# A Perceiver kernel: the last three running maxima of a half batch ahead of the span attention's minimum on VectorE, and the first block's copy ahead of the deferred steps on ScalarE

## The chip, the cores and the metric

The kernel runs on one core of one Trainium2 chip. The metric is the device time of one execution in microseconds. The time before is the median of three runs. The profile is of one further execution, with a time of its own; every duration below is from that execution.

## The reference, cut to what matters

There are 32 batches of 64 queries with 256 features. Each batch attends to its own 1601 context rows with 16 heads of width 16, then goes through a second, "span" attention over its own 64 positions, then through a hash-routed mixture of small networks:

```python
x = x + xattn(layernorm(x), ctx, ctx, mask)     # softmax over 1601 keys, 16 heads
x = x + span_attn(layernorm(x))                 # below
x = x + ffn(layernorm(x))                       # shared network + 2 of 8 experts per token
# span_attn, per head: mean and soft are made from h @ W_span.T
diff = pos[None, None, :] - mean[..., None]
scores = -soft[..., None] * (diff * diff)       # 64 positions for each of 64 queries
attn = softmax(scores); out = attn @ value
```

Both softmaxes take off a maximum before the exponential. In the span attention the kernel holds soft·diff², so the maximum of the scores is the minimum of that tensor; the kernel calls it `least`.

## The kernel before, in words

A **half** is one batch with 8 of its 16 heads; there are 64 halves, numbered n = 0 to 63, and the loop over them is the main part of the program. The scores of a half lie in SBUF with keys on the partitions, as 13 blocks of 124 keys; for each block there are four pairs of heads, 128 columns each. The 13 blocks are worked in four groups (4, 3, 3 and 3 blocks). The loop is a software pipeline: in turn n the scores of half n+1 are made, the maxima of half n are subtracted, its exponentials are taken, and the products with the values of half n-1 are made. A turn has four **stretches**, one for each group; stretch 4n+g is group g of turn n.

The order of instructions on TensorE, VectorE, ScalarE and GpSimd is the order in which the program issues them (a manual schedule), so moving a call in the source moves its instructions in the queues of exactly those engines that it uses.

In one stretch VectorE adds the mask to four tiles of scores (L504, out of PSUM into `prob`), and between these adds it takes running maxima over blocks that are already there (`maximum`, L525, 124x512, into the PSUM tile `mrun`). The running maximum starts as a copy of block 0, made by ScalarE (`first_maxima`, L517). Blocks 1 to 9 are taken between the adds; blocks 10, 11 and 12 are taken at the end of the turn (`BETWEEN[-1]`, L745), and the last of them writes `mx` instead of `mrun`. At the start of the next turn TensorE turns `mx` (four transposes into `pm`, L532), VectorE reduces that to `mc` (L539), TensorE spreads `mc` over the rows (`pb`, L547), ScalarE copies that to `mb` (L551), and GpSimd subtracts `mb` from each pair of heads (`less_maxima`, L556), 3.7 us each. TensorE's order around this is: scores of group 0 (`psc`, L495), `pm`, one key projection of the next batch (`pk`, L450), `pb`, 104 products with values (`pvs`, L571), scores of group 1.

The span attention of a tile of two batches is a generator, `span_steps`, whose parts are put into an **agenda**: `run(s)` at stretch s runs the next part of every generator due there, and the list `WAITS` says how many stretches later the following part is due. A tile starts every four halves, so each part of it comes at the same place of every fourth turn. In turns 6, 10, 14, ... 62 (15 of them) these parts come up:
- group 0: the small VectorE arithmetic (L279 to L295), which borrows a corner of `mrun` as scratch through `aside`. The first block's copy, L517, overwrites that corner and so must come later.
- group 2: ScalarE's square and GpSimd's product (L304, L305).
- group 3: VectorE's `least` (L308, 128x1024 reduced to 128x16) and GpSimd's subtraction of it (L309).

In the turn after (7, 11, ...) group 0 has ScalarE's exponential of the span scores (L311), and group 1 has VectorE's `total` (L313). In the following turn, group 0 has the transposes and the two copies `aT` (L325); in the one after that, group 0 has the last sum of one tile (`po`, L343 and L346) and the copy `hT` (L228) of the next. ScalarE's `qbd` and the normalisations stand in other groups. The `run` call of group 3 stands before the three last maxima, and the `run` call of group 0 before the first block's copy.

Of the kernel before, what the change touches and what calls it, by code (L numbers as in the profile page):

```python
# [33 lines left out]
BETWEEN = [(), (1, 2, 3), (4, 5, 6), (7, 8, 9), (10, 11, 12)]  # L34
# [40 lines left out]
def perceiver_kernel(ctx: ExitStack, tc: tile.TileContext, a: dict[str, bass.AP], out: bass.AP):  # L75
# [3 lines left out]
    NTILE = NT // P  # L79
# [130 lines left out]
    WAITS = (1, 1, 1, 1, 1, 1, 1, 1, 1, 1, 1, 3, 3, 1, 1, 1)  # L210
    CLOSE = (1, 1, 1, 1, 0, 2, 1, 1, 1, 1, 1, 2, 1, 1, 1, 1)

    def span_steps(t: int, oT):
        waits = iter(CLOSE if t >= NTILE - 2 else WAITS)
        x = xs[t]
        po = mm_bank(f"po_{t}")
        for c in range(2):
# [101 lines left out]
        for q in range(2):  # L319
            ps = mm_bank(f"psa_{t}_{q}")  # L320
            for i in range(4):
                n = 4 * q + i
# [6 lines left out]
        for c in range(2):  # L329
            for b in range(2):  # L330
                for j in range(4):
                    n = 4 * c + j
# [46 lines left out]
    def pair_of(n: int, j: int):  # L379
        return prob[:CHUNK, place(n, j // 2), j % 2]  # L380

    def block_of(n: int, k: int):

        first, last = place(n, 0), place(n, 1)
        return prob[:CHUNK, first : last + 1 : last - first, :, k, :]
# [23 lines left out]
    def query_steps(t: int):  # L409
        spread = spread_of(xs[t], f"q{t}")  # L410
        yield 1
        xn = normalised(xs[t], spread, f"q{t}")
        yield 1
        ps = transposed(xn, f"q{t}")
        xnT = work.tile([P, 2, P], F32, tag="xnT", name=f"xnT_{t}")
        nc.vector.tensor_copy(xnT, ps)
        yield 1
        pq = mm_bank(f"pq_{t}")
        for c in range(2):
            for i in range(2):  # L420
                nc.tensor.matmul(
                    pq[:, c * P : (c + 1) * P], lhsT=wqT[:, i, c * P : (c + 1) * P],
                    rhs=xnT[:, i, :], start=(i == 0), stop=(i == 1),
                )

        q = work.tile([P, 2, 2, 2, S], F32, tag="qbd", name=f"qbd_{t}")
        for c in range(2):
            for e in range(2):
                nc.scalar.activation(
                    q[:, c, :, e, :], pq[:, c * P : (c + 1) * P].rearrange("p (b q) -> p b q", b=2),  # L430
                    AF.Identity, bias=bq4[:, c, e : e + 1], scale=own4[:, e : e + 1],
                )
        qbd[t] = q
        yield 1

        nc.gpsimd.tensor_tensor(xs[t], xs[t], bo_row, ALU.add)

    def load_context(b: int):
        for g in range(len(GROUPS)):
            load_piece(b, g)  # L440
        if b % 2 == 0 and b // 2 + 1 < NTILE:
            t = b // 2 + 1
            load_x(t)
# [72 lines left out]
    def first_maxima(n: int):  # L516
        nc.scalar.copy(mrun[:CHUNK].rearrange("p (r i) q -> p r i q", r=2), block_of(n, 0))  # L517

    def maximum(n: int, k: int):

        dst = mrun
        if k == NKC - 1:
            dst = mxs[n] = work.tile([P, 4, P], F32, tag="mx", bufs=1, name="mx")
        dst, run = (m[:CHUNK].rearrange("p (r i) q -> p r i q", r=2) for m in (dst, mrun))
        nc.vector.tensor_tensor(dst, block_of(n, k), run, ALU.max)  # L525

    def turned_maxima(n: int):

        m = mxs.pop(n)
        ps = mm_bank("pm")  # L530
        for j in range(4):
            nc.tensor.transpose(  # L532
                ps[:, j * CHUNK : (j + 1) * CHUNK], m[:CHUNK, j, :], ident[:CHUNK, :CHUNK]
            )
        return ps, work.tile([P, 4], F32, tag="mc", name="mc")
# [7 lines left out]
    def maxima_along_rows(col):  # L543

        ps = mm_bank("pb")
        for j in range(4):
            nc.tensor.transpose(  # L547
                ps[:CHUNK, j * P : (j + 1) * P], col[:, j : j + 1].to_broadcast([P, CHUNK]), ident
            )
        m = work.tile([P, 4, P], F32, tag="mb", bufs=1, name="mb")  # L550
        nc.scalar.copy(m[:CHUNK].rearrange("p j q -> p (j q)"), ps[:CHUNK])  # L551
        return m

    def less_maxima(n: int, j: int, m, engine):
        sj = pair_of(n, j)
        engine.tensor_tensor(  # L556
            sj, sj, m[:CHUNK, j, None, :].to_broadcast([CHUNK, NKC, P]), ALU.subtract
        )

    def exponentials(n: int, j: int):  # L560
        nc.scalar.activation(pair_of(n, j), pair_of(n, j), AF.Exp)  # L561

    def values(n: int, r: int):

        b, c = halves[n]
        v = vs[b % 2]
        for k in range(NKC):
            kn = min(CHUNK, KEYS - k * CHUNK)
            for j in range(4):
                h = 4 * r + j  # L570
                nc.tensor.matmul(  # L571
                    pvs[32 * j : 32 * j + DK + 1, c, :, r, :],
                    lhsT=v[:kn, k, 8 * c + h, :],
                    rhs=pair_of(n, h // 2)[:kn, k, (h % 2) * S : (h % 2) * S + S],
                    start=(k == 0), stop=(k == NKC - 1), tile_position=(0, 32 * j),
                )
# [51 lines left out]
            nc.vector.scalar_tensor_tensor(at, p3, b3twice[:, hc : hc + 1], act, ALU.add, ALU.mult)  # L628

    agenda: dict[int, list] = defaultdict(list)  # L630

    def run(stretch: int):
        for steps in agenda.pop(stretch, []):
            while (wait := next(steps, None)) == 0:
                pass
            if wait:
                agenda[stretch + wait].append(steps)

    def finish_steps(b: int, stretch: int):

        t = b // 2
        if b % 2 == 0:
            oT[t] = work.tile([P, 2, 2, S], F32, tag="oT", name=f"oT_{t}")
        flat = "p c u r q -> p (c u r q)"
        nc.vector.transpose(turned_pvs.rearrange(flat), pvs.rearrange(flat))
        by_head = turned_pvs.rearrange("p c u r i -> p (c u r) i")
        rec = work.tile([P, 8], F32, tag="rec", name=f"rec_{b}")
        nc.vector.reciprocal(rec, by_head[:, :, DK])
        o = work.tile([P, 8, DK], F32, tag="o", name=f"o_{b}")
        nc.vector.tensor_tensor(  # L650
            o, by_head[:, :, :DK], rec[:, :, None].to_broadcast([P, 8, DK]), ALU.mult
        )
        nc.vector.transpose(oT[t][:, :, b % 2, :], o.rearrange("p (c n) i -> p c (n i)", c=2))
        if b % 2:
            agenda[stretch + 1].append(span_steps(t, oT.pop(t)))
        yield


# [37 lines left out]
    for n, (b, c) in enumerate(halves[:-1]):  # L696
        if c == 0 and b + 1 < B:
            load_context(b + 1)
        if c and b % 2 == 0 and b // 2 + 1 < NTILE:
            agenda[4 * n + 2].append(query_steps(b // 2 + 1))  # L700

        def project(f, *args):
            if b + 1 < B:
                f(b + 1, *args)

        if n:
            values(n - 1, 0)
            exponentials(n - 1, 3)
        for g in range(len(GROUPS)):
            if g == 0:  # L710
                turned = []

                def turn():
                    turned.extend(turned_maxima(n))
                    return turned

                scores(n + 1, g, BETWEEN[g], turn)
                project(project_keys, c, 0)
                m = maxima_along_rows(turned[1])
                less_maxima(n, 0, m, nc.gpsimd)  # L720
                run(4 * n)
                if n:
                    values(n - 1, 1)
                    if c == 0:
                        agenda[4 * n + 1].append(finish_steps(b - 1, 4 * n + 1))
            else:
                scores(n + 1, g, BETWEEN[g])
                project(project_keys, c, g, g == 3)
                if g == 1:
                    project(project_values, 3 * c)  # L730
                elif g == 2:
                    project(project_values, 3 * c + 1)
                else:
                    for u in (5, 6) if c else (2,):
                        project(project_values, u, True)
            if g:
                less_maxima(n, g, m, nc.gpsimd)
                run(4 * n + g)
            for u in extra.get(4 * n + g, ()):
                linear_factor(u)  # L740
            if g == 0:
                first_maxima(n + 1)
            else:
                exponentials(n, g - 1)
        for k in BETWEEN[-1]:  # L745
            maximum(n + 1, k)


    stretch = 4 * last
# [13 lines left out]
    run(stretch + 1)  # L763
    values(last, 1)
    next(finish_steps(B - 1, stretch + 3))
    gate()
    gate()
# [155 lines left out]
```

## Time and profile before

| what | value |
|---|---|
| runs before | median 1583.82 us (1578.76 to 1586.79, three runs) |
| the profiled execution's own time | 1575.67 us |
| its span, first to last instruction | 1573.6 us |
| mean granted TensorE clock | 0.993 |
| TensorE busy, and weight loads | 1499.1 us (95%), 1094.7 us (70%) |
| VectorE busy | 1258.5 us (80%) |
| GpSimd busy | 1121.5 us (71%) |
| ScalarE busy | 895.6 us (57%) |

The first turn begins at about 40 us, and the last maxima of the last half end at 1409.6 us; what follows is the tail with the last tiles and the mixture of networks. A timeline row gives start, duration, engine, line, operation, output<-inputs, shapes and count; in square brackets is the time for which the engine was idle before it, and what ended that. Rows that follow each other on one engine can overlap by about 0.1 us.

### The profile page before, as it was taken

How to read it: one execution, taken by the hardware profiler on the slowest of the kernel's cores; microseconds unless marked ns; L12 is line 12 of the kernel's file. 1: busy time of each engine (PE TensorE's matmuls, PEld its weight loads, DVE VectorE, ACT ScalarE, POOL GpSimd, SP SyncE). 2: the span in 40 equal slices, each digit the busy share in tenths (PEclk: the TensorE clock that was granted, in tenths of full speed). 3: DMA queues.
4: the chain of work that ended last, by engine and by line, in shares of the span. 5: the costliest groups of instructions: out<-in, count | busy, mean ns of one | idle time of the engine just before them, and what ended most of it. 6: DMA issues, size and time to landing. Idle time of an engine off the chain costs nothing.

```text
span 1573.6 us, 61215 instructions
## 1 busy us (share of the span) xinstructions
PE 1499.1 (95%) x27856; PEld 1094.7 (70%) x27856; DVE 1258.5 (80%) x2700; ACT 895.6 (57%) x1229; POOL 1121.5 (71%) x424
## 2 busy tenths in 40 slices
PE   8999999999999999999999999999999999988899
PEld 5677776776767676776767677767767676754587
DVE  4888889888888988898888988898888889884200
ACT  3565656665565656665666656566655656555311
POOL 1777877878687877788786977778786878761710
PEclk9999999999999999999999999999999999999999
DMA  5111111111111111111111111111111111004100
GB/s 167 55 42 43 35 39 38 44 51 44 51 44 51 32 42 35 46 39 44 51 44 52 44 38 35 41 35 44 51 44 52 44 47 33 6 2 155 57 27 27
DMA packets 52066, 73.68 MB, mean 47 GB/s; under 512 B 3812, under 2 KB 51040, under 8 KB 51680
## 3 DMA queue, kind: packets, MB, share of 16 engines
q1 hardware_dynamic: 50992, 69.00, 15.2%
q8 instruction: 218, 3.57, 0.9%
q10 hardware_dynamic: 816, 0.79, 0.1%
q14 instruction: 40, 0.33, 0.1%
HBM read 65.57 MB, written 4.19 MB: 44 GB/s over the span
## 4 chain that ended last, share of the span: by engine, by line
PE 55%; DVE 41%; issue 2%; ACT 1%; POOL 1%; DMA 0%; DVEq 0%; ACTq 0%; POOLq 0%
DVE mrun L525 15%; DVE prob L504 15%; PE pk L450 13%; PE pv L450 11%; PE psc L495 8%; PE pvs L571 8%; PE py L853 4%; PE u L600 3%; PE pm L532 2%; PE ph L835 2%; PE pb L547 1%; DVE mx L525 1%; DVE total L313 1%; DVE least L308 1%; DVE mrun L293 1%
## 5 line engine op out<-in xcount | busy, mean ns | idle before, releaser
L556 POOL TENSOR_TENSOR prob<-prob,mb 124x1664 f32<-124x1664 f32 x252 | 936.5, 3735 | 274.1 <-ACT mb L551 186.2
L504 DVE TENSOR_TENSOR prob<-psc,madd 124x384 f32<-124x384 f32 (+1 forms) x1024 | 568.6, 581 | 146.1 <-PE psc L495 146.1
L525 DVE TENSOR_TENSOR mrun<-prob,mrun 124x512 f32<-124x512 f32 x704 | 483.7, 687 | 3.9
L561 ACT ACTIVATE prob<-prob 124x1664 f32<-124x1664 f32 x256 | 403.3, 1588 | 46.7 <-POOL prob L556 43.7
L450 PE MATMUL pk<-ct,wkT_sb 128*32 128x361 f32 (+2 forms) x1768 | 406.0, 499 | 8.0 <-DMA wkT_sb<-in_wkT 5.4
L450 PE MATMUL pv<-wvT_sb,ct 128*124 128x256 f32 x3524 | 390.9, 379 | 0.0
L450 PEld LDWEIGHTS pv<-wvT_sb,ct 128*124 128x124 f32 x3524 | 273.5, 132 | 119.8 <-issue 16.8
L465 ACT ACTIVATE kT<-pk,cols 128x372 f32<-128x372 f32 (+2 forms) x256 | 151.9, 593 | 224.8 <-PE pk L450 224.6
L495 PE MATMUL psc<-qbd,kT 32*124 32x128 f32 x6656 | 267.9, 284 | 12.1 <-DVE prob L504 8.5
L495 PEld LDWEIGHTS psc<-qbd,kT 32*124 32x124 f32 x6656 | 214.3, 181 | 65.6 <-DVE prob L504 26.4
L450 PEld LDWEIGHTS pk<-ct,wkT_sb 128*32 128x32 f32 (+1 forms) x1768 | 159.0, 145 | 117.8 <-issue 53.1
L482 ACT COPY v<-pv 124x512 f32<-124x512 f32 (+1 forms) x224 | 124.8, 557 | 202.6 <-PE pv L450 202.4
L571 PE MATMUL pvs<-prob,v 124*17 124x64 f32 x13312 | 212.5, 220 | 1.1 <-issue 0.9
L571 PEld LDWEIGHTS pvs<-prob,v 124*17 124x17 f32 x13312 | 195.7, 98 | 21.1 <-issue 10.8
L532 PE MATMUL pm<-cst,mx 124*128 124x124 f32 x256 | 41.1, 284 | 38.5 <-DVE mx L525 38.0
L517 ACT COPY mrun<-prob 124x512 f32<-124x512 f32 x64 | 38.5, 602 | 59.5 <-DVE soft L295 56.4
L855 DVE SCALAR_TENSOR_TENSOR ot<-py,prob 128x256 f32<-128x256 f32 x16 | 6.8, 425 | 75.7 <-PE py L853 75.7
L600 PE MATMUL u<-xfT,sw_sb 128*128 128x512 f32 x128 | 61.4, 630 | 1.3 <-ACT vbd L262 0.9
L532 PEld LDWEIGHTS pm<-cst,mx 124*128 124x128 f32 x256 | 26.8, 142 | 48.4 <-DVE mx L525 29.6
L547 PEld LDWEIGHTS pb<-cst,mc 128*124 128x124 f32 x256 | 30.0, 136 | 36.1 <-DVE mc L539 25.5
L600 PEld LDWEIGHTS u<-xfT,sw_sb 128*128 128x128 f32 x128 | 25.0, 203 | 30.6 <-issue 26.2
L525 DVE TENSOR_TENSOR mx<-prob,mrun 124x512 f32<-124x512 f32 x64 | 43.9, 686 | 2.2
(126 smaller groups left out, 1128.9 us busy)
## 6 DMA issues: line engine op xcount, KB each, us to landing
ct<-in_ctxT SPq DMA_DIRECT2D x64, 372.0 KB, 3.2
ct<-in_ctxT SPq DMA_DIRECT2D x32, 496.0 KB, 3.6
ct<-in_ctxT SPq DMA_DIRECT2D x32, 361.0 KB, 3.2
w<-in_w SPq DMA_DIRECT2D x16, 256.0 KB, 5.9
x<-in_x SPq DMA_DIRECT2D x16, 128.0 KB, 2.6
x_kept<-x SPq DMA_DIRECT2D x16, 128.0 KB, 2.4
prob<-x_kept SPq DMA_DIRECT2D x8, 256.0 KB, 6.1
out<-ot SPq DMA_DIRECT2D x16, 128.0 KB, 1.9
```

Of the source, the lines that this page charges most:

```text
L450: nc.tensor.matmul(out[at:end], lhsT=lhsT[:, at:end], rhs=rhs, start=start, stop=stop, **(dict(tile_position=(0, at)) if tiled else {}),)
L465: nc.scalar.activation(kTs[c][:, k0 : k0 + kn], ps[:, :kn], AF.Identity, bias=cols[:, B_K + c : B_K + c + 1])
L482: nc.scalar.copy(vs[b % 2][:kn, 2 * u : 2 * u + n, :, :DK], ps[:kn, : n * D].rearrange("p (n h d) -> p n h d", n=n, d=DK),)
L495: nc.tensor.matmul(ps[:CHUNK, k * P : (k + 1) * P], lhsT=kTs[c][32 * j : 32 * j + 32, at : at + CHUNK], rhs=qbd[b // 2][32 * j : 32 * j + ...
L504: nc.vector.tensor_tensor(pair_of(n, j)[:, c0 : c0 + nb, :].rearrange("p k (e q) -> p k e q", e=2), ps[:CHUNK, : nb * P].rearrange("p (k e ...
L525: nc.vector.tensor_tensor(dst, block_of(n, k), run, ALU.max)
L532: nc.tensor.transpose(ps[:, j * CHUNK : (j + 1) * CHUNK], m[:CHUNK, j, :], ident[:CHUNK, :CHUNK])
L556: engine.tensor_tensor(sj, sj, m[:CHUNK, j, None, :].to_broadcast([CHUNK, NKC, P]), ALU.subtract)
L561: nc.scalar.activation(pair_of(n, j), pair_of(n, j), AF.Exp)
L571: nc.tensor.matmul(pvs[32 * j : 32 * j + DK + 1, c, :, r, :], lhsT=v[:kn, k, 8 * c + h, :], rhs=pair_of(n, h // 2)[:kn, k, (h % 2) * S : ( ...
L600: nc.tensor.matmul(ps, lhsT=w[:, c, hc * P : (hc + 1) * P], rhs=xfT[:, c, :, slot], start=(c == 0), stop=(c == 1),)
L853: nc.tensor.matmul(py, lhsT=x, rhs=w, start=(n == 0), stop=(n == len(terms) - 1))
```

## The change

Two calls move. The three last maxima (`BETWEEN[-1]`) now come inside group 3, ahead of `less_maxima` and `run(4 * n + 3)`, instead of after the exponentials. The first block's copy (`first_maxima`) now comes ahead of `run(4 * n)` and of the second half of the value products, except in those turns whose group 0 uses the scratch corner of `mrun`; a set `held_at` remembers them. `finish_steps` fills that set when it puts a tile's generator into the agenda, by summing the tile's first six waits.

```diff
+    SMALL = 6
+
+    def waits_of(t: int):
+        return CLOSE if t >= NTILE - 2 else WAITS
...
-        waits = iter(CLOSE if t >= NTILE - 2 else WAITS)
+        waits = iter(waits_of(t))
...
+    held_at: set = set()
...
             agenda[stretch + 1].append(span_steps(t, oT.pop(t)))
+            held_at.add(stretch + 1 + sum(waits_of(t)[:SMALL]))
...
                 less_maxima(n, 0, m, nc.gpsimd)
+                if 4 * n not in held_at:
+                    first_maxima(n + 1)
                 run(4 * n)
...
+            if g == 3:
+                for k in BETWEEN[-1]:
+                    maximum(n + 1, k)
             if g:
                 less_maxima(n, g, m, nc.gpsimd)
                 run(4 * n + g)
...
             if g == 0:
-                first_maxima(n + 1)
+                if 4 * n in held_at:
+                    first_maxima(n + 1)
             else:
                 exponentials(n, g - 1)
-        for k in BETWEEN[-1]:
-            maximum(n + 1, k)
```

In the built program this changes the following, and nothing else in any queue. On VectorE, in 15 places, the sequence "maximum of block 9, `least`, maxima of blocks 10, 11, 12" becomes "maxima of blocks 9, 10, 11, 12, `least`". On ScalarE, in 43 places, the copy L517 passes ahead of its neighbours: 15 times ahead of `hT` (L228), 14 times ahead of the span exponential (L311), and 14 times ahead of the two copies `aT` (L325). The orders on TensorE, GpSimd and the DMA queue stay as they are.

## The prediction

> **What bounds the kernel now.** I read the page's chain of waits first, then the timeline around one place where an order changes, then the granted clock around several of them. The chain:
>
> ```profile
> PE 55%; DVE 41%; issue 2%; ACT 1%; POOL 1%; DMA 0%; DVEq 0%; ACTq 0%; POOLq 0%
> ```
>
> TensorE and VectorE take turns; ScalarE and GpSimd are almost never what the end waits for. So a moved ScalarE instruction is free unless it is made late by more than its slack, and a moved VectorE instruction counts where VectorE hands over to TensorE. One of the 15 places (the maxima of half 39, timeline of all engines):
>
> ```profile
> 879.44 1.21 DVE L308 TENSOR_REDUCE least<-sc 128x16 f32<-128x1024 f32 x1
> ...
> 880.56 1.42 DVE L525 TENSOR_TENSOR mrun<-prob,mrun 124x512 f32<-124x512 f32 x2
> 882.01 0.69 DVE L525 TENSOR_TENSOR mx<-prob,mrun 124x512 f32<-124x512 f32 x1
> 882.51 1.90 POOL L309 TENSOR_TENSOR sc<-sc,least 128x1024 f32<-128x1024 f32 x1
> ...
> 882.61 1.28 DVE L504 TENSOR_TENSOR prob<-psc,madd 124x512 f32<-124x512 f32 x2
> ...
> 882.75 0.64 PE L532 MATMUL pm<-cst,mx 124*128 124x124 f32 x4 [1.74 <-DVE mx L525]
> ...
> 883.23 1.83 PE L450 MATMUL pk<-ct,wkT_sb 128*128 128x496 f32 x4
> ...
> 883.81 0.67 DVE L539 TENSOR_REDUCE mc<-pm 128x4 f32<-128x496 f32 x1
> ...
> 884.90 0.60 PE L547 MATMUL pb<-cst,mc 128*124 128x128 f32 x4
> ...
> 886.14 1.07 ACT L311 ACTIVATE sc<-sc 128x1024 f32<-128x1024 f32 x1
> 886.33 7.41 POOL L556 TENSOR_TENSOR prob<-prob,mb 124x1664 f32<-124x1664 f32 x2 [1.92 <-ACT mb L551]
> ...
> 887.10 0.60 ACT L517 COPY mrun<-prob 124x512 f32<-124x512 f32 x1
> ...
> 887.96 1.02 DVE L504 TENSOR_TENSOR prob<-psc,madd 124x384 f32<-124x384 f32 x2 [2.29 <-PE psc L495]
> ```
>
> TensorE stands idle for 1.74 us because `mx` is behind `least`. The wait is the same to 0.01 us in all 14 places inside the loop (maxima of halves 7, 11, ... 59). But look at what follows: `mc` has its own condition on VectorE (two adds before it), and `pb` needs it.
>
> **The maxima ahead of the minimum.** Without `least` in between, the same four maxima look like this (half 37):
>
> ```profile
> 834.59 2.14 DVE L525 TENSOR_TENSOR mrun<-prob,mrun 124x512 f32<-124x512 f32 x3
> 836.77 0.69 DVE L525 TENSOR_TENSOR mx<-prob,mrun 124x512 f32<-124x512 f32 x1
> 837.37 1.28 DVE L504 TENSOR_TENSOR prob<-psc,madd 124x512 f32<-124x512 f32 x2
> ```
>
> From the first maximum's start to the end of `mx` it is 836.77 + 0.69 - 834.59 = 2.87 us; with `least` it is 882.70 - 878.84 = 3.86 us. So `mx` comes 0.99 us earlier and `pm` starts at about 881.76. `pk` then ends at 884.07 instead of 885.06. That is not the gain. The next thing late is `mc`: VectorE still does the four maxima, `least`, two adds and then `mc`, in whatever order. Its sum even grows. A maximum that depends on the one before starts 0.72 us after it (three in 2.14 us and the next at 2.18); `least` depends on none of them and starts 0.60 us after one. With `least` in the middle, the step to the first add is 882.61 - 878.84 = 3.77 us; after the change it is the 2.78 us of half 37 (837.37 - 834.59) plus the step of `least`, 880.56 - 879.44 = 1.12, together 3.90. So `mc` ends 0.13 us later, at 884.61. Where `pb` really waits for `mc`, at half 62, it ends 0.77 us after it:
>
> ```profile
> 1387.88 0.67 DVE L539 TENSOR_REDUCE mc<-pm 128x4 f32<-128x496 f32 x1
> ...
> 1388.69 0.62 PE L547 MATMUL pb<-cst,mc 128*124 128x128 f32 x4 [1.53 <-DVE mc L539]
> ```
>
> (1389.31 against 1388.54 within rounding.) So `pb` ends at 884.61 + 0.77 = 885.38 instead of 885.50: 0.12 us gained, and the value products, the scores of group 1 and VectorE's add at 887.96 move by as much. In 14 places: **1.7 us**. The idle time of TensorE is not gone: 0.75 us of it stays before `pm` (881.76 against the 881.01 at which the scores ended) and 0.7 us comes to stand before `pb` (884.76 against 884.07).
>
> [...]
>
> What else hangs on `least`: GpSimd's L309 behind it starts at 882.9 (`least` then ends at about 882.8) instead of 882.51 and ends 0.4 us later; the subtraction queued behind it waits for `mb` anyway, with 1.92 us of idle time, so this is covered down to 1.5 us. The span exponential L311 on ScalarE, now at 886.7, comes 1.9 us after that. `least` itself waits for L305, which ended at 878.86. Cost nothing.
>
> The fifteenth place is the end of the loop (half 63): TensorE idles 3.59 us before `pm` at 1409.74, no `pk` is there, and `mc` waits for `pm`. There the 0.99 us of `mx` passes through to `mb` and the chain behind: **1.0 us**, between 0 and 1.1 (the clock there is at half, and which rows fall under it may shift).
>
> **The copy ahead of the steps.** The copy takes 0.60 us, needs the four adds of group 0 (done at 885.67 here) and follows `mb`, which ends at 886.25. Its reader is VectorE's first maximum at 888.90, which did not wait. So nothing is gained by having it earlier. What it delays: L311 by 0.6 us, to 887.8, read by `total` at 891.62 (3.8 us of slack); `hT`, which waits for TensorE 0.37 us in half 37 while the copy now fills that gap, by about 0.1; the two `aT` copies by 0.6, whose reader on TensorE comes three stretches later. If a bank of PSUM that `hT` or `aT` free were wanted at once, the cost would be up to 0.6 us in 29 places, 17 us; but at half 40 the late `aT` would end at 907.75 (now 907.15) and the next scores start at 907.87, and `hT` has over 1 us. I take 0 for the 43 places.
>
> **The clock.** The last view is the granted clock in windows:
>
> ```profile
> core 0: us, PE busy (x) PEld busy (x) DVE busy (x) ACT busy (x) POOL busy (x), PEclk, DMA share, GB/s
> ...
> 1054.40:1057.80 3.40, 1.66 (x65) 1.36 (x53) 3.33 (x6) 1.43 (x2) 3.40 (x2) 1.00 0.02 5
> 1057.80:1061.20 3.40, 3.40 (x8) 1.84 (x8) 2.76 (x5) 1.26 (x1) 1.50 (x1) 0.50 0.00 0
> ...
> 1231.90:1235.30 3.40, 1.66 (x37) 1.33 (x30) 3.33 (x6) 1.42 (x2) 3.40 (x2) 1.00 0.02 5
> ```
>
> After one of the 14 waits (half 47) TensorE ran at half clock for 3.4 us; `pk` took 3.25 us instead of 1.83, and `pb` came 3.84 us after `pm` instead of 2.15: **1.69 us** lost. The same wait at 1231.9, lying elsewhere in its window, cost nothing. [...] The half-clock stretches of this trace (1057.8, 1409.4, 1436.7 and 1464.0 us) do lie whole multiples of 3.41 us apart; but the gap that preceded the first was 1.74 us. [...] With the change the longest idle time there is 0.75 us, less than the 0.81 us before `pm` in half 37 and its like, after none of which the clock fell; a window that catches both new gaps has about 1.3 us of idle time in its 3.41 and so 2.1 us busy, against 1.66 now. So the falls inside the loop should go.
>
> How many there are in another run depends on where its windows lie. Places follow each other by 87.06 us (882.70 - 795.64), 25.5 windows. A fall adds 1.69 us, which makes 88.75 us, 26.0 windows: the next place then meets the same part of a window, and can fall again. So one run may have one fall and another a row of them. The median run is 1583.82 - 1575.67 = 8.15 us above the profiled one, which is 4.8 such falls, and the three runs differ by 8.0 us among themselves. I can't see these runs, so this is an inference.
>
> **The sum.** Against the profiled execution: 1.7 + 1.0 + 1.7 = 4.4 us, so a span of 1569.2 and, with the 2.07 us around it, 1571.3 us. Against the median: 1583.82 - 2.7 = 1581.1 without falls, less 1.69 for each fall in the median run. With four falls, between the one seen and the six that would explain all of the 8 us, it is 1574.4. I forecast **1574 us**.
>
> **The rivals.**
> - Falls are rare in every run, and the 8 us between profile and runs are something else that stays. For it: 13 of 14 waits passed at full clock. Against it: the spread of the runs. Gain 2.7 to 4.4 us: 1579.4 to 1581.1 us, say 1580.
> - The change does nothing at all: `pb` waits for `mc` as long as it did for `pk`, and falls come elsewhere. This needs 0.12 us more on `mc`. 1583.8 us.
> - Slower: the gap before `pm` of 0.8 us in the halves 9, 13, ... 61 starts to let the clock fall, because removing the larger falls leaves the windows lying badly for all of them. Price 1.69 us each; it decides once it happens more than about six times a run beyond today's falls (2.7 + 7.9 us = 6.3 x 1.69). With all 14: 1583.8 - 2.7 + 23.7 = 1604.8; with eight, 1594.6. Against it: none fell in the profile.
>
> **How the numbers follow.** I give the forecast 0.50, the first rival 0.36, no effect 0.07, slower 0.07. About 0.5% (7.9 us) is what a measurement of this kernel can tell from no change. The forecast needs a median of 1575.9 or less for that; with three falls it is just missed (2.7 + 5.1 = 7.8), so I count 0.45 of it as faster and 0.05 within; with the rivals, within 0.5% is 0.48 and slower 0.07. The forecast's own range is 1571 to 1577; with the first rival and no effect it reaches from 1570 to 1584.
>
> **What would show it.** Right: TensorE's wait for `mx` drops from 1.74 to about 0.75 us in the 14 places, a wait of about 0.7 us for `mc` appears before `pb`, VectorE's idle time before the group 1 add goes from 2.29 to about 2.2, no half-clock window lies between 100 and 1400 us, and the runs after differ by less than 8 us. Wrong: half-clock windows still in the loop, `mc` ending earlier than reckoned, a wait for L517's neighbours on TensorE, or `total` waiting for L311.

## The result, and the profile after

The changed kernel takes 1568.69 us (median of six runs, 1565.35 to 1572.28). The kernel before, run beside it and together with the runs shown above, takes 1582.78 us (1578.76 to 1587.61). The ratio is 0.9908, with a 95% interval of 0.9884 to 0.9932. In a second comparison, described below, it is 0.9951 (0.9932 to 0.9969). The direction was forecast; the time lies 1.3 us below the forecast range of 1570 to 1584 us. The later comparisons have more runs and give smaller differences, 7.5 us for the changed kernel and 9.2 us for the moved maxima alone: a good part of the first one's 14.1 us comes from its runs of the kernel before, which lie high.

The profiled execution after takes 1565.35 us, its span is 1563.2 us: 10.4 us less than before. The page's chain of waits and two of its groups after, and behind them the first of the groups before:

```profile
PE 53%; DVE 43%; issue 2%; ACT 1%; POOL 1%; DMA 0%; DVEq 0%; POOLq 0%; ACTq 0%
...
L537 PE MATMUL pm<-cst,mx 124*128 124x124 f32 x256 | 40.3, 280 | 23.6 <-DVE mx L530 23.5
...
L552 PE MATMUL pb<-cst,mc 128*124 128x128 f32 x256 | 39.4, 277 | 10.9 <-DVE mc L544 10.9
```

```profile
L532 PE MATMUL pm<-cst,mx 124*128 124x124 f32 x256 | 41.1, 284 | 38.5 <-DVE mx L525 38.0
```

(Lines of the code are 5 to 11 further down: `maximum` is L530, `least` L313, `mc` L544, `pb` L552, the first block's copy L522.) TensorE's idle time before `pm` fell from 38.5 to 23.6 us in total, and the wait for `mc` before `pb` grew from 2.3 to 10.9 us. The same place as before, half 39, in the timeline (first the row of before that the distances below start from, then the changed kernel):

```profile
878.84 0.69 DVE L525 TENSOR_TENSOR mrun<-prob,mrun 124x512 f32<-124x512 f32 x1
```

```profile
876.94 2.14 DVE L530 TENSOR_TENSOR mrun<-prob,mrun 124x512 f32<-124x512 f32 x3
...
879.12 0.69 DVE L530 TENSOR_TENSOR mx<-prob,mrun 124x512 f32<-124x512 f32 x1
879.72 1.21 DVE L313 TENSOR_REDUCE least<-sc 128x16 f32<-128x1024 f32 x1
879.86 0.64 PE L537 MATMUL pm<-cst,mx 124*128 124x124 f32 x4 [0.76 <-DVE mx L530]
...
881.01 1.90 POOL L314 TENSOR_TENSOR sc<-sc,least 128x1024 f32<-128x1024 f32 x1 [0.37 <-DVE least L313]
882.05 0.66 DVE L544 TENSOR_REDUCE mc<-pm 128x4 f32<-128x496 f32 x1
...
882.76 0.65 PE L552 MATMUL pb<-cst,mc 128*124 128x128 f32 x4 [0.59 <-DVE mc L544]
...
884.17 3.73 POOL L561 TENSOR_TENSOR prob<-prob,mb 124x1664 f32<-124x1664 f32 x1 [1.25 <-ACT mb L556]
...
885.87 1.02 DVE L509 TENSOR_TENSOR prob<-psc,madd 124x384 f32<-124x384 f32 x2 [1.97 <-PE psc L500]
```

The wait before `pm` is 0.76 us, and 0.59 us of wait stands before `pb`. From the start of the first maximum to the end of `mc` it is 5.77 us (882.71 - 876.94) against 5.64 before (884.48 - 878.84), 0.13 us more; to the end of `pb` it is 6.47 against 6.66, 0.19 less. From the maxima of half 35 to those of half 39 it is 86.85 us (879.80 - 792.95) against 87.06 (882.70 - 795.64): a place is worth 0.21 us (0.20 by the unrounded times).

The granted clock in two long windows, first of the kernel before, then of the changed one (columns: stretch, its length, busy time of the five engines with their instructions, clock, DMA share, GB/s):

```profile
100.00:1400.00 1300.00, 1250.34 (x25432) 917.83 (x25431) 1139.12 (x2460) 791.75 (x1077) 1020.82 (x353) 1.00 0.15 42
1400.00:1562.00 162.00, 148.75 (x1042) 104.83 (x1041) 47.48 (x100) 55.25 (x85) 50.28 (x45) 0.95 0.19 62
```

```profile
100.00:1400.00 1300.00, 1256.20 (x25486) 917.94 (x25488) 1144.62 (x2469) 794.88 (x1080) 1025.92 (x355) 1.00 0.15 42
1400.00:1562.00 162.00, 146.79 (x1038) 106.75 (x1026) 44.22 (x94) 51.69 (x81) 45.45 (x43) 0.99 0.20 65
```

In the tail the clock is 0.95 before and 0.99 after. A **fall** is a stretch in which the clock is at half; the trace's clock records show it in windows of 3.41 us. Before, one such window lies in the loop and five in the tail; after, none in the loop and one in the tail.

So the 10.4 us of the two profiles divide as follows. The last `mx` ends at 1403.78 instead of 1409.59 us, 5.8 us earlier: 14 x 0.21 = 2.9, one fall in the loop 1.7, and 1.0 from the wait at the end of the loop (2.60 us instead of 3.59), which makes 5.6. That the sum fits so well is in part luck: from `mx` of half 7 to that of half 59, what the 13 periods of four halves take above the shortest of them, apart from the fall, comes to 3.9 us before and 4.0 after, but to 6.9 in a second profile of the changed kernel, which has no fall in the loop either. The tail after it takes 159.4 instead of 164.0 us, 4.6 less. The runs below say which of this belongs to the change.

### The profile page after: what moved, and what is told of

Its sections match the earlier page's. It is cut to its first block, busy times and chain, and to the rows that moved or that the text cites. A ratio compares the mean times of both kernels' runs of the same rounds, so it can differ in the third digit from the quotient of the medians.

```text
span 1563.2 us, 61201 instructions
## 1 busy us (share of the span) xinstructions
PE 1494.7 (96%) x27856; PEld 1089.8 (70%) x27856; DVE 1259.5 (81%) x2700; ACT 895.3 (57%) x1229; POOL 1121.7 (72%) x424
## 4 chain that ended last, share of the span: by engine, by line
PE 53%; DVE 43%; issue 2%; ACT 1%; POOL 1%; DMA 0%; DVEq 0%; POOLq 0%; ACTq 0%
DVE prob L509 16%; DVE mrun L530 15%; PE pk L455 11%; PE pv L455 11%; PE pvs L576 8%; PE psc L500 8%; PE py L864 4%; PE u L605 2%; PE ph L846 2%; PE pb L552 2%; PE pm L537 1%; DVE least L313 1%; DVE total L318 1%; DVE mc L544 1%; DVE mrun L298 1%
## 5 line engine op out<-in xcount | busy, mean ns | idle before, releaser
L530 DVE TENSOR_TENSOR mrun<-prob,mrun 124x512 f32<-124x512 f32 x704 | 483.6, 687 | 4.4
L522 ACT COPY mrun<-prob 124x512 f32<-124x512 f32 x64 | 38.2, 598 | 59.3 <-DVE soft L300 56.2
L537 PE MATMUL pm<-cst,mx 124*128 124x124 f32 x256 | 40.3, 280 | 23.6 <-DVE mx L530 23.5
L552 PEld LDWEIGHTS pb<-cst,mc 128*124 128x124 f32 x256 | 28.7, 135 | 48.1 <-DVE mc L544 41.2
L605 PE MATMUL u<-xfT,sw_sb 128*128 128x512 f32 x128 | 57.9, 600 | 1.3 <-ACT vbd L267 0.9
L552 PE MATMUL pb<-cst,mc 128*124 128x128 f32 x256 | 39.4, 277 | 10.9 <-DVE mc L544 10.9
L530 DVE TENSOR_TENSOR mx<-prob,mrun 124x512 f32<-124x512 f32 x64 | 44.0, 687 | 2.2
```

What stands on the lines that cost most here:

```text
L537: nc.tensor.transpose(ps[:, j * CHUNK : (j + 1) * CHUNK], m[:CHUNK, j, :], ident[:CHUNK, :CHUNK])
L552: nc.tensor.transpose(ps[:CHUNK, j * P : (j + 1) * P], col[:, j : j + 1].to_broadcast([P, CHUNK]), ident)
L605: nc.tensor.matmul(ps, lhsT=w[:, c, hc * P : (hc + 1) * P], rhs=xfT[:, c, :, slot], start=(c == 0), stop=(c == 1),)
```

## Experiments

Two theories stood against each other. By the theory of the clock, most of the gain in the median comes from falls of TensorE to half clock that follow the 1.74 us wait for `mx`, and the order itself gives 4 us. By the rival, the order on VectorE, or the copy, gives the gain and the clock is incidental. Kernels that were measured together share the runs of the kernel before.

### The three maxima alone

```diff
+            if g == 3:
+                for k in BETWEEN[-1]:
+                    maximum(n + 1, k)
             if g:
                 less_maxima(n, g, m, nc.gpsimd)
...
-        for k in BETWEEN[-1]:
-            maximum(n + 1, k)
```

> The three last maxima move ahead of the minimum; the copy on ScalarE stays where it was. If the copy is worth nothing, as the prediction says: the whole gain of the change, a ratio to the kernel before of 0.991 (0.988 to 0.993). If the copy carries a part of the gain: between 0.993 and 1.000. In the profile the wait before pm in the 14 places is 0.76 us and the idle time before the group 1 add 1.97 us, as in the changed kernel.

Measured: 1569.40 us (11 runs) against 1578.61 (31 runs), ratio 0.9941 (0.9922 to 0.9961). The wait before `pm` is 0.76 us (once 0.75) in the 14 places, and no window of the loop was at half clock. The ratio forecast for it was too far down, because the kernel before is faster in these runs than in the six above; the median is within 0.7 us of the changed kernel's.

### The copy alone

The edit is the change without the two hunks on `BETWEEN[-1]`:

```diff
                 less_maxima(n, 0, m, nc.gpsimd)
+                if 4 * n not in held_at:
+                    first_maxima(n + 1)
                 run(4 * n)
...
             if g == 0:
-                first_maxima(n + 1)
+                if 4 * n in held_at:
+                    first_maxima(n + 1)
```

> The copy on ScalarE moves; the maxima stay behind the minimum. If the copy is worth nothing: 0.999 to 1.001, the wait before pm stays at 1.74 us in all 14 places, and half-clock windows in the loop stay possible. If the copy carries a part of the gain: 0.993 to 0.998.

Measured: 1579.37 us (14 runs) against 1578.61, ratio 1.0003 (0.9983 to 1.0023). The copy is worth nothing. The waits stayed at 1.74 to 1.75 us, and this profile caught three falls in the loop, each directly after such a wait:

```profile
184.60:188.00 3.40, 3.40 (x8) 1.93 (x9) 2.81 (x5) 1.29 (x1) 1.52 (x1) 0.50 0.04 10
273.30:276.70 3.40, 3.40 (x8) 1.93 (x9) 2.82 (x5) 1.42 (x1) 1.66 (x1) 0.51 0.00 0
1235.90:1239.30 3.40, 3.40 (x8) 1.89 (x8) 2.77 (x5) 1.36 (x1) 1.60 (x1) 0.50 0.00 0
```

Eight matmuls fill each of these windows, most of them the last transposes and the key projection, at a clock of 0.50 to 0.51.

### The order of before, with the wait filled

```diff
         ps = mm_bank("pm")
+        for _ in range(3 if n % 4 == 3 and 7 <= n < 60 else 0):
+            nc.tensor.matmul(ps[:, :D], lhsT=ident, rhs=wvT[:, 0, :], start=True, stop=True)
```

> The kernel before, with three more matmuls of 128x256 on constants put on TensorE ahead of the four transposes into pm in the 14 places (about 1.3 us of its 1.74 us wait); they write what the transposes overwrite. The order on VectorE stays. Theory of the clock (falls to half clock after these waits make most of the gain in the median): mx, pm and the group 1 add stay at the same distance from each other as before, no half-clock window lies between 100 and 1400 us, and the time falls by 4 to 7 us, a ratio of 0.996 to 0.9975. Rival (the order on VectorE makes the gain, the clock little): 0.9995 to 1.001, or slower by the matmuls if they delay pm.

Measured: 1571.63 us (13 runs) against 1578.61, ratio 0.9957 (0.9936 to 0.9978), just past the far end of what was expected (0.996). TensorE in its timeline, at half 39:

```profile
881.34 1.56 PE L532 MATMUL pm<-wvT_sb,cst 128*128 128x256 f32 x6
883.15 0.64 PE L534 MATMUL pm<-cst,mx 124*128 124x124 f32 x4 [0.25 <-DVE mx L525]
883.63 1.83 PE L450 MATMUL pk<-ct,wkT_sb 128*128 128x496 f32 x4
885.30 0.60 PE L549 MATMUL pb<-cst,mc 128*124 128x128 f32 x4
```

Useless matmuls stand in the wait, and `pb` still comes 2.15 us after `pm`, as before; VectorE's wait in group 1 is still 2.29 us. No step of the work is earlier at such a place, yet the kernel is 7.0 us faster, and its profile has no half-clock window in the loop. That is the theory of the clock.

### One matmul in place of three

```diff
-        for _ in range(3 if n % 4 == 3 and 7 <= n < 60 else 0):
+        for _ in range(1 if n % 4 == 3 and 7 <= n < 60 else 0):
```

> The kernel before with one constant matmul in place of three in the 14 waits, which leaves about 1.3 us of the 1.74 us idle. Half 5 of the loop waits 1.16 us and never fell in a profile. If a wait of 1.3 us is also too short to fall after: the same as with three matmuls, a ratio of 0.996, and a granted clock of 0.995 to 0.999. If it still falls at some positions: between 0.997 and 1.000 and a clock between.

Measured: 1570.95 us (21 runs) against 1577.56 (25 runs), ratio 0.9954 (0.9936 to 0.9971), the granted clock 0.994 to 0.999 (mean 0.996). The lower end is 0.001 outside what was expected. What is left of the wait:

```profile
881.24 0.70 PE L532 MATMUL pm<-wvT_sb,cst 128*128 128x256 f32 x2
883.06 0.64 PE L534 MATMUL pm<-cst,mx 124*128 124x124 f32 x4 [1.12 <-DVE mx L525]
```

So a wait of 1.12 us does no harm here and one of 1.74 us can.

Which of the 1.74 us waits are followed by a fall can be read from the traces. Within one trace the falls begin whole multiples of 3.413 us apart, so they give a grid of windows. The profiles of the kernel before and of the copy alone hold 28 such waits: the four that ended 3.23 to 3.30 us into a window were followed by a fall, and the 24 that ended anywhere from 0.08 to 2.77 us into one were not. Here are two waits of the kernel before, one of each kind (the falls of that profile begin at 1057.82 and 1409.40 us; the waits end 3.23 and 2.59 us into their windows):

```profile
1057.64 0.95 PE L532 MATMUL pm<-cst,mx 124*128 124x124 f32 x4 [1.74 <-DVE mx L525]
...
1234.49 0.64 PE L532 MATMUL pm<-cst,mx 124*128 124x124 f32 x4 [1.74 <-DVE mx L525]
```

TensorE is busy for 1.66 us in both windows (the rows in the prediction), so it is not the busy time alone that decides; why the place in the window does is open. With one matmul in the wait, three waits of 1.12 us ended 3.16, 3.18 and 3.32 us into a window, and no fall followed: these passed by their shorter wait, not by a luckier place.

### The minimum taken twice

```diff
+        if t < NTILE - 2:
+            nc.vector.tensor_reduce(small("again"), sc, AX.X, ALU.min)
         nc.vector.tensor_reduce(least, sc, AX.X, ALU.min)
```

> The kernel before with the span minimum taken twice in the 14 places (the first result is not used), so that mx is 1.12 us later and TensorE waits about 2.86 us. The order alone costs 14 x 1.12 = 15.7 us, since pm, pk and pb follow mx. Theory of the clock: a longer wait falls at more positions of the window, so 8 to 14 places of a run fall instead of about 4, at 1.4 to 1.7 us each: 1599 to 1611 us, and a granted clock of 0.980 to 0.987 instead of 0.992. Rival (the falls do not depend on this wait): 1592 us at the clock of the kernel before.

Measured: 1608.97 us (5 runs) against 1577.56, ratio 1.0178 (1.0129 to 1.0226), 31.4 us more, of which the order explains 15.7. The clock of its runs is 0.977 to 0.985. In the profile 10 of the 14 waits, now 2.86 us each, were followed by a fall, three of them by two windows. The first of these:

```profile
core 0: us, PE busy (x) PEld busy (x) DVE busy (x) ACT busy (x) POOL busy (x), PEclk, DMA share, GB/s
269.30:272.70 3.40, 1.29 (x48) 1.00 (x36) 3.34 (x4) 1.34 (x2) 3.40 (x2) 1.00 0.02 5
272.70:276.10 3.40, 2.64 (x7) 1.67 (x8) 3.39 (x6) 1.15 (x1) 1.39 (x1) 0.50 0.00 0
276.10:279.50 3.40, 3.40 (x43) 1.98 (x45) 0.35 (x1) 1.37 (x3) 0.04 (x1) 0.50 0.16 20
```

With 1.12, 1.74 and 2.86 us of wait the profiles of the order of before had 0, then 1 and 3, then 10 places with a fall, of 14. The rival's 1592 us is 10 us below the fastest run.

### The changed kernel again, and the wait at the end of the loop

Four kernels ran together: the changed kernel; the kernel before with its 14 waits filled and seven matmuls in the 3.6 us wait at the end of the loop; the changed kernel with five matmuls in its 2.6 us wait there; and one more, told last. The edit of the second; the third has `5 if n == last else 0` as its count:

```diff
+        for _ in range(7 if n == last else 3 if n % 4 == 3 and n >= 7 else 0):
+            nc.tensor.matmul(ps[:, :D], lhsT=ident, rhs=wvT[:, 0, :], start=True, stop=True)
```

> The changed kernel itself, beside the following ones. If a whole number of half-clock windows at about 1.7 us each makes the difference from run to run: its slowest and fastest runs lie under 8 us apart, at granted clocks of 0.994 to 0.999, and no half-clock window of its profile lies between 100 and 1400 us. Ratio 0.991 to 0.995. Rival (a gain that has nothing to do with the clock): the ratio does not depend on the clocks of the runs of the kernel before.

Measured: 1568.71 us (15 runs, 1563.94 to 1572.97) against 1576.17 (48 runs, 1568.70 to 1586.81), ratio 0.9951 (0.9932 to 0.9969). The range of 9.0 us is wider than the 8 expected; the clocks are 0.994 to 0.999, as expected, and the loop has no half-clock window.

> The kernel before with constant matmuls in the 14 waits of the loop (three each) and in the 3.6 us wait at the end of the loop (seven). It keeps the order on VectorE and takes away both kinds of long idle time on TensorE. Theory of the clock: the half-clock windows that follow 1409 us go or become fewer too; the time is 1 to 4 us below the filled loop alone, about 1567 to 1570 us. Rival: the same as with the filled loop alone, 1571.6 us.

Measured: 1571.25 us (22 runs), ratio 0.9958 (0.9943 to 0.9973). That is the rival's answer: filling the end of the loop adds nothing to the filled loop (1571.63). The fall at 1409 us is gone from its profile, but four half-clock windows begin at 1427, 1437 and 1465 us all the same.

> The changed kernel with five constant matmuls in its 2.6 us wait at the end of the loop. Its loop has no falls, so what it is below the kernel before with both waits filled is the order alone: 14 x 0.21 + 1.0 = 3.9 us by the profile. Against the changed kernel: 1 to 3 us faster if the tail's half-clock windows begin at that wait, nothing if they begin later.

Measured: 1568.24 us (17 runs), ratio 0.9951 (0.9933 to 0.9969). It is 3.0 us below the kernel before with both waits filled, against 3.9 reckoned. Two kernels without falls in the loop and with the end filled differ by the order alone; so the order is worth about 3 us (the spread of these runs leaves about 1 to 5). TensorE at the end of the loop, first with the order of before, then with the changed one:

```profile
1409.51 0.64 PE L534 MATMUL pm<-cst,mx 124*128 124x124 f32 x4 [0.29 <-DVE mx L525]
1410.92 0.65 PE L549 MATMUL pb<-cst,mc 128*124 128x128 f32 x4 [0.77 <-DVE mc L541]
```

```profile
1402.19 0.64 PE L539 MATMUL pm<-cst,mx 124*128 124x124 f32 x4 [0.15 <-DVE mx L530]
1403.91 0.65 PE L554 MATMUL pb<-cst,mc 128*124 128x128 f32 x4 [1.07 <-DVE mc L546]
```

In the changed order `least` stands between `mx` and `mc` here too: `pb` starts 1.72 us after `pm` instead of 1.41. So 0.3 of the 1.0 us gained at `mx` is given back, 0.7 is left at the end of the loop, and the order comes to 14 x 0.21 + 0.7 = 3.6 us by the profiles. In this comparison, then, the medians go from 1576.17 to 1571.25 us by filling the waits and to 1568.24 by the order: 4.9 us for the falls and 3.0 for the order.

The filling of the end itself, 0.5 us, is less than was expected and less than these runs can tell. It does act on the clock: in all nine profiles that leave the wait there as it is, 2.60 or 3.59 us, a fall began in it or behind it (before at 1409.40 us, 0.34 us ahead of its end; after at 1405.82 us, 1.90 us behind its end), and in none of the three that fill it. But those three have other falls later in the tail.

The granted clock was taken with every run. Over the 104 runs of the kernel before that were made beside these kernels, time and clock have a correlation of -0.94; the fitted line is 1.40 us for each 0.001 of clock. One window of 3.41 us at half clock is 0.0011 of the mean over 1575 us, so a fall costs about 1.5 us by the line; 1.69 us was read at half 47. The means by clock, with the changed kernel's 21 runs beside:

| granted clock of the run | before: runs, mean time | changed: runs, mean time |
|---|---|---|
| 0.997 and up | 12, 1571.9 us | 10, 1567.1 us |
| 0.994 to 0.996 | 24, 1574.2 us | 11, 1570.5 us |
| 0.991 to 0.993 | 32, 1577.8 us | none |
| 0.985 to 0.990 | 36, 1583.1 us | none |

At equal clock the changed kernel is 3.7 to 4.8 us faster; the rest of the gain is that runs at low clock no longer occur. The mean clock is 0.9922 over the 104 runs and 0.9964 over the 21: about four half-clock windows fewer.

### The minimum behind `mc`

The waits within the changed kernel, so that `least` comes in group 0 of the next turn, after the four adds (the span exponential and `total` come one stretch later with it):

```diff
-    WAITS = (1, 1, 1, 1, 1, 1, 1, 1, 1, 1, 1, 3, 3, 1, 1, 1)
+    WAITS = (1, 1, 1, 1, 1, 1, 1, 1, 2, 1, 1, 2, 3, 1, 1, 1)
```

> The changed kernel, with the span minimum put one stretch later, into group 0 of the next turn, behind the four adds and mc (waits of 2, 1, 1, 2 in place of 1, 1, 1, 3 around it), for the tiles 0 to 13. If mc behind the minimum is what keeps the gain of a place at 0.2 us, then here mx and mc are both about 1 us earlier than before: the add of group 1 comes 0.99 us earlier than in the kernel before, 0.78 us earlier than in the changed one, 10.9 us in 14 places: a ratio of 0.984 to 0.985 to the kernel before. If something else (GpSimd, whose subtraction of the minimum now stands between two of its subtractions of mb, or the products' order) sets the place, the ratio stays at 0.990 or worse.

Measured: 1563.92 us (6 runs, 1558.50 to 1566.85) against 1578.61, ratio 0.9908 (0.9878 to 0.9938). It beats both kernels, but the ratio is the one expected if something else sets the place. Against the maxima alone, measured beside it, it is 5.5 us less, half of the 10.9 expected. VectorE at the same place:

```profile
877.42 0.69 DVE L530 TENSOR_TENSOR mx<-prob,mrun 124x512 f32<-124x512 f32 x1
...
881.00 1.21 DVE L313 TENSOR_REDUCE least<-sc 128x16 f32<-128x1024 f32 x1
...
883.37 1.02 DVE L509 TENSOR_TENSOR prob<-psc,madd 124x384 f32<-124x384 f32 x2 [1.16 <-PE psc L500]
...
887.41 1.02 DVE L509 TENSOR_TENSOR prob<-psc,madd 124x384 f32<-124x384 f32 x2 [0.29 <-PE psc L500]
```

From the end of `mx` (878.11) to the group 1 add it is 5.26 us, as in the kernel before (887.96 - 882.70), with `mx` 0.99 us earlier: so the full 0.99 us is there, and `least` lies in VectorE's idle time. In the next group VectorE meets TensorE, which has the scores only 0.29 us later. From that add to the next half's `mx` it takes 14.97 us (898.34 - 883.37) instead of 14.59 (902.55 - 887.96), so 0.38 us are given back, 0.29 of them in this wait. Since `total` has left this stretch of VectorE for the next, where it still takes its 1.2 us, the wait may belong to the moved `total` as much as to the moved minimum; no run parts the two. A period is 86.43 us: 0.62 below before, 0.42 below the changed kernel, about 5.8 us in 14 places.

The same, with five constant matmuls at the end of the loop as above:

```diff
+        for _ in range(5 if n == last else 0):
+            nc.tensor.matmul(ps[:, :D], lhsT=ident, rhs=wvT[:, 0, :], start=True, stop=True)
```

> The minimum behind mc, and five constant matmuls in the wait at the end of the loop. By the profiles 14 x 0.43 = 6.0 us below the changed kernel with the same filling; about 1558 to 1561 us, a ratio of 0.986 to 0.989 to the kernel before.

Measured: 1563.39 us (5 runs), ratio 0.9906 (0.9871 to 0.9940), 2.4 us above what was expected and the same as without the filling within what these runs can tell. Against the changed kernel with the same filling (1568.24) it is 4.9 us less, of the 6.0 expected.

## Why the prediction was right or wrong

**The maxima ahead of the minimum: right, and slightly too small.** That the gain would stop at `mc`, that `mc` would end 0.13 us later, and that the wait before `pm` would be 0.75 us, all came out to 0.01 us. The term that was mis-sized is "ends 0.77 us after it", taken from half 62: from the end of `mc` to the end of `pb` it is 0.70 us in these places. Of the 0.09 us by which the place is better than forecast (0.21 instead of 0.12), that explains 0.07; the rest is within rounding. Over 14 places it is 2.9 instead of 1.7 us. The 0.13 us comes from the two steps in the rows, 0.72 us behind a maximum that the next one needs and 0.60 us behind one that `least` does not need; had they been equal, `mc` would not have moved.

**The end of the loop: right for `mx`, wrong behind it.** The wait for `mx` shrank by 0.99 us, as forecast. That all of it "passes through to `mb`" failed: `mc` waits for `least` there as in the other places, and 0.7 us is left.

**The copy: right.** No gain, no loss: 1.0003.

**The clock: right in its cause, wrong in its size.** The falls in the loop went, as forecast. That the busy time of a window decides, as the comparison of 2.1 with 1.66 us has it, was an estimate and was not shown; what the runs show is the length of the wait and its place in the window. The step that failed is "With four falls, between the one seen and the six that would explain all of the 8 us, it is 1574.4". The base of that sum, 1583.82 us, and the number of falls were not free of each other. The 104 later runs of the kernel before have a median of 1577.4 us, and only 22% of them are as slow as 1582.78; so the three runs lay at the slow end. That they held more falls than usual is inferred from this, since their clocks are not on record. With the 5.8 falls that their distance from the profile implied, the same sum gives 1583.82 - 2.7 - 9.8 = 1571.3; with the 3.6 us of order it is 1570.4, inside the changed kernel's runs and 1.7 us above their median. For the usual run, four falls were right: the clocks of the later runs say about four. Against those runs, 8.7 us (1577.4 - 1568.7) were gained, and the forecast 9.4 (four falls at 1.69 and 2.7 of order) is close to that, in part by luck: the order was taken too small and the fall, at 1.5 us by the fitted line, too dear. I lowered an inference by a third and kept the base that it came from.

**The tail: not forecast.** Of the two profiles' difference, 4.6 us lie in the tail, with five half-clock windows before and one after. The profiles do not give this to the change: that of the maxima alone, with the same order in the tail, has four such windows, the changed kernel's second profile one, and the kernel before with a filled loop one. How the windows fall in the tail differs from run to run.

**The rivals.** That falls are rare is refuted by the clocks of the runs; that nothing happens, by both ratios. The slower case did not come: in no profile of the changed order did the clock fall after a wait of 0.8 us.

**The windows' regularity** (a fall at one place makes the next place meet the same part of a window) was argued from the distances 25.5 and 26.0. It came out once in four. Of the four falls in the loops of the two profiles with 1.74 us waits, one was followed by a fall at the next place, 26.0 windows later (184.59 and 273.34 us with the copy alone). After the other three the next wait came 89.1 instead of 88.75 us later, ended about 0.2 us into a window, and no fall followed. That the falls come at one place of the window is seen in these traces; that they come in long rows is not.

## What to carry to other kernels

- Before a median is taken as the base of a sum, ask what differs from run to run, and put the base and the assumed cause at the same point: here the granted clock of a run told its time with a correlation of -0.94.
- A wait of TensorE had a second price here beside its length: at half 47, where the clock fell after 1.74 us of wait, `pb` came 1.69 us later. Filling the waits with useless matmuls took 4.9 us off the median, the reordering of the work on the path 3.0, so look at the clock behind a wait too.
- When an instruction is moved off a hand-over, look for the next hand-over on the same engine. Behind `mx` stood `mc`, and 0.8 of the 1.0 us was lost there; with `least` out of its way, 0.4 was lost in the next group.

## What the runs showed of the hardware

- A wait of TensorE of 1.74 us was followed by 3.41 us at half clock in 4 of 28 places, with the same instructions around it: in those where it ended 3.23 to 3.30 us into a 3.41 us window, and in none where it ended up to 2.77 us into one. Of 14 waits of 1.12 us none was followed by a fall, of 14 waits of 2.86 us ten were.
- Filling the 14 waits of 1.74 us with matmuls on constants, down to 0.25 us each, made the kernel 7.0 us faster; at a place without a fall no step of its work was earlier.
- On VectorE a 124x512 maximum of 0.69 us that reads the result of the one before started 0.72 us after it (kernel before, half 37: three in 2.14 us, `mx` 2.18 us after the first); `least`, which reads none of them, started 0.60 us after one (half 39 before, 878.84 and 879.44; after, 879.12 and 879.72).
